# Dealing a tile's deep blocks over the whole batch, in a sparse graph attention on one core

## The chip, the core and the metric

The kernel runs on one core of a Trainium2 chip. The metric is the device time of one execution in microseconds; the median of three runs of the kernel before is 1906.26 us (1904.83 to 1914.43). TensorE (PE) does matrix products, VectorE (DVE) and ScalarE (ACT) elementwise work and reductions, GpSimd (POOL) issues indirect DMAs (gathers and scatters by a list of rows) and SyncE (SP) plain DMAs. Each engine runs its own list of instructions in the order in which the program emitted them and waits for the others by semaphores.

## What is computed

Attention over the edges of a graph, then the output projection, the residual and a layer norm, for 16 batches of 1024 nodes of 512 numbers, 8 heads of 64, all in fp32:

```python
q = (x @ Wq + bq).reshape(b, n, H, HD)
k = (x @ Wk + bk).reshape(b, n, H, HD)
v = (x @ Wv + bv).reshape(b, n, H, HD)
scores = einsum('bqhd,bkhd->bhqk', q, k) / sqrt(HD)
scores = scores + (1.0 - adj)[None, None] * -1e9
attn = softmax(scores, axis=-1)
out = einsum('bhqk,bkhd->bqhd', attn, v).reshape(b, n, d)
return layernorm(x + out @ Wo + bo)
```

`adj` (1024 x 1024, zeros and ones) is the same for all batches and very sparse: most nodes have a handful of edges, a few have dozens.

## The kernel before

**Tiles and blocks.** The nodes are sorted by their number of edges and cut into eight tiles of 128 queries, tile 7 having most edges. The kernel never makes the 1024 x 1024 scores. It works in *blocks* of 128 pairs of a query and a key. An *own* block i of tile t holds the i-th edge of each of its 128 queries; `OWN = (2, 1, 2, 3, 4, 5, 5, 7)` says how many each tile has. Edges beyond these are packed densely, 128 at a time, into *deep* blocks, `BLOCKS = (0, 0, 0, 0, 0, 0, 1, 5)`: tile 6 has one, tile 7 has five. Tiles 0 to 5 are called short here. Tile 1 (one key for each query) has no softmax to do and is handled apart; from the third batch on (`PAIRED_FROM = 2`) tile 0 is done once for two batches, in the odd one. So a batch has 34 blocks, or 32 in the even batches from 2 on, and the program has 530.

**What a block costs.** The list `blocks` fixes the order of all blocks, and one loop walks it, step n for block n, emitting for several blocks at once at different stages:

- `gather(n + 8)`: POOL gathers the K and V rows of the 128 keys (`kvg`, L1242, 128 x 1024); for a deep block also the 128 query rows (`qg`, L1196); at a tile's first block SP loads its query tile (`qt`).
- `products(n + 4)` (`qk`, L1263) and `scores(n + 4)` (`s`, L1267): VectorE multiplies Q and K and adds up by head.
- `exponentials(n + 3)` (`pv`, L1278): ScalarE.
- `weigh`: V times the exponentials, either on ScalarE as eight activations, one a head (L1291, at step n for block n + 2), or on VectorE as one operation (L1295, for block n + 1). `by_act(n)` decides. Own blocks after a tile's first always go to ScalarE; deep blocks go by turns (batch number plus i); a tile's first block goes by whether its place n in the list is even. The last 34 blocks go to VectorE where there is a choice.
- own blocks: `add_own(n)` (L1307), VectorE adds to the tile's running sum. Deep blocks: `add_up(n)`, two PE products with a matrix of zeros and ones (`sum`, L1316 and L1317) that send each edge to its query, accumulated in one pair of PSUM banks (a single buffer, `sum`) over the tile's deep blocks.
- `normalise(b, t)`, the closing of a tile: VectorE divides by the sum of exponentials (L1336, L1337), for tiles 6 and 7 after adding the `sum` buffer (L1328, L1329). Four PE transposes (`poT`, L1351), a copy by ScalarE (`oT`, L1355) and the output projection (`po`, L790) follow, then residual, layer norm and the store.

**The other work of the loop.** Meanwhile PE computes Q, K and V of the batches ahead, the *fronts*: transposes of x (`pxT`), products with Wq (`pq`), and K and V by a scheme with seven products in place of eight (`x`, `pp`, `z`, L947), whose results VectorE and ScalarE combine (L774 to L777 before the products, `e` L960, `w` L963, `g` L966, `kv` L970, L975, L979 and L826 after). K and V go to memory as rows, from which the gathers read; the Q rows likewise, into one of three buffers.

**What sets PE's share of a step.** Each step adds to a `credit`, and front or projection units are emitted while it lasts. `paced(share, n)` deals it over the steps of a batch in the ratio of `load_of(n)`, the planner's count of VectorE operations in the step: 2, plus 1 if the next block is weighed on VectorE, plus 1 for an own block that is not a tile's first, plus 1.3 at the step after a short tile closed or 3.0 after a deep one. An `add_up` takes `SUM` off the credit.

**The order before.** `blocks_of(b, t)` gives the order within a tile, and the list was simply tile after tile. For tile 6 that is 0 1 2 *5* 3 4, for tile 7 it is 0 1 *7* 2 *8* 3 *9* 4 *10* 5 *11* 6 (deep blocks slanted). So the five deep blocks of tile 7 all stood in the last 12 of a batch's 34 (or 32) blocks. A tile was closed at the step in which the next tile's block 0 came up. The one-key tile is turned at tile 7's own block 4, and its values are gathered at tile 7's block 0 (for the last batch both at tiles 2 and 3).

Of the kernel before, what the change touches and what calls it, by code (L numbers as in the profile page):

```python
# [26 lines left out]
OWN = (2, 1, 2, 3, 4, 5, 5, 7)  # L27
BLOCKS = (0, 0, 0, 0, 0, 0, 1, 5)
# [6 lines left out]
LONE, ONE_KEY, ONE_KEY_AT, ONE_KEY_LAST = 64, 1, (7, 4), (3, 0)  # L35
# [3 lines left out]
PAIRED_FROM, SPARED = 2, 56  # L39
# [138 lines left out]
def kernel(  # L178
# [37 lines left out]
    B, N, D = x.shape  # L216
    HD = D // HEADS
    NPAIR = D // P
    NT = N // P
# [34 lines left out]
    with ExitStack() as main:  # L254
# [82 lines left out]
        def merged(b):  # L337
            return b >= PAIRED_FROM and b % 2 == 1

        def tiles_of(b):  # L340
            return [t for t in range(NT) if t or b < PAIRED_FROM or merged(b)]
# [832 lines left out]
        def blocks_of(b, t):  # L1174

            own, deep = list(range(OWN[t])), list(range(OWN[t], OWN[t] + BLOCKS[t]))
            if b == 0 or not deep:
                return own + deep
            spread = max(1, len(own) // (len(deep) + 1))
            left = len(own) - spread * len(deep)  # L1180
            for j, i in enumerate(deep):
                own.insert(left + j * (spread + 1), i)
            return own

        blocks = [(b, t, i) for b in range(B) for t in tiles_of(b) if t != ONE_KEY for i in blocks_of(b, t)]
        start = [min(n for n, block in enumerate(blocks) if block[0] == b) for b in range(B)] + [len(blocks)]

        def load_more():
# [3 lines left out]
        def one_key_at(b):  # L1192
            return ONE_KEY_AT if b < B - 1 else ONE_KEY_LAST
# [71 lines left out]
        def scores(n):  # L1265
            S[n] = small.tile([P, HEADS], F32, tag="s", name=f"s_{n}", bufs=4)
            nc.vector.tensor_reduce(S[n], QK.pop(n).rearrange("p (h d) -> p h d", d=HD), axis=AX.X, op=OP.add)  # L1267
# [12 lines left out]
        def by_act(n):  # L1280
            b, t, i = blocks[n]
            if 0 < i < OWN[t]:
                return True
            turn_of = b + i if b and i else n
            return n < total - NBT and (turn_of % 2 == 0 or n < NBT // 2)
# [33 lines left out]
        def normalise(b, t):  # L1319
            pv = PV.pop((b, t))  # L1320
            o = work.tile([P, D], F32, tag="o", name=f"o_{b}_{t}", bufs=2)
            order_of = [u for u in tiles_of(b) if u != ONE_KEY]
            if t == order_of[0]:
                RDEN[b] = small.tile([P, NT - 1, HEADS], F32, tag="rden", name=f"rden_{b}", bufs=1)[:, 0:len(order_of), :]
            r = RDEN[b][:, order_of.index(t), :]
            if BLOCKS[t]:
                s = PSUM.pop((b, t))
                nc.vector.tensor_tensor(r, s[:, 1, HD2:HD2 + HEADS], pv[:, D:], op=OP.add)  # L1328
                nc.vector.tensor_tensor(  # L1329
                    o.rearrange("p (a d) -> p a d", a=2), s[:, :, 0:HD2], pv[:, 0:D].rearrange("p (a d) -> p a d", a=2),  # L1330
                    op=OP.add,
                )
                nc.vector.reciprocal(r, r)
                pv = o
            else:
                nc.vector.reciprocal(r, pv[:, D:])  # L1336
            nc.vector.tensor_tensor(  # L1337
                o.rearrange("p (h d) -> p h d", d=HD), pv[:, 0:D].rearrange("p (h d) -> p h d", d=HD),
                r[:, :, None].to_broadcast([P, HEADS, HD]), op=OP.mult,
            )  # L1340
            turn(b, t, o)
            if t == NT - 1:
                r = RDEN.pop(b)
                for k, op in enumerate((OP.min, OP.max)):
                    nc.vector.tensor_reduce(ends[:, k, b:b + 1], r, axis=AX.XY, op=op)

        def turn(b, t, o):
            def transpose():
                p = fill_psum(f"poT_{b}_{t}")
                for c in range(NPAIR):  # L1350
                    nc.tensor.transpose(p[:, ts(c, P)], o[:, ts(c, P)], ident)  # L1351

                def out():
                    OT[b, t] = work.tile([P, D], F32, tag="oT", name=f"oT_{b}_{t}", bufs=LAZY + 2)
                    nc.scalar.copy(OT[b, t], p)  # L1355
                    if number(b, t) in SPILL:
                        later(1, lambda: nc.sync.dma_start(spill[b * NT + t], OT.pop((b, t))))
                        spilled.append((b, t))
                    else:
                        later(1, lambda: done.append((b, t)))  # L1360

                later(1, out)

            later(1, lambda: urgent.append(transpose))
            if not fronts:
                coming.append((b, t))
# [67 lines left out]
        total = len(blocks)  # L1434
# [4 lines left out]
        def load_of(n):  # L1439

            b, t, i = blocks[n]
            had = 2.0 + (not by_act(min(n + 1, total - 1))) + (0 < i < OWN[t])
            if i == 0:
                had += 3.0 if BLOCKS[blocks[n - 1][1]] else 1.3
            return had

        def paced(share, n):
            if n >= total:
                return share
            b = blocks[n][0]  # L1450
            return share * load_of(n) * (start[b + 1] - start[b]) / sum(load_of(m) for m in range(start[b], start[b + 1]))
# [11 lines left out]
        with tc.manual_schedule():  # L1463
# [20 lines left out]
            n = -LEAD_IN  # L1484
            while n < total or plan or rest or urgent or done or finishing or spilled or lone_tiles or not guarded:
# [6 lines left out]
                elif n in start:  # L1492

                    b = start.index(n)
# [15 lines left out]
                    add_own(n)  # L1510
                if 0 <= n + 4 < total:
                    scores(n + 4)
                if 1 <= n <= total and (n == total or blocks[n][2] == 0):
                    normalise(*blocks[n - 1][:2])
                if 0 <= n < total and blocks[n][1:] == one_key_at(blocks[n][0]):
                    turn(blocks[n][0], ONE_KEY, V1.pop(blocks[n][0]))
                if 0 <= n < total and blocks[n] == (B - 1, *MORE_AT):
# [87 lines left out]
```

## Time and profile before

| | |
|---|---|
| median of three runs | 1906.26 us |
| the profiled execution | 1894.52 us, its span 1892.4 us |
| stretch from batch 1's closing to batch 14's | 394.9 to 1761.4 us |
| in it: PE, VectorE, ScalarE, POOL busy | 1338.6, 1272.7, 1196.4, 938.8 us |
| in it: DMA share | 0.88 |
| before and after that stretch | 394.9 us and 131.0 us |

All times that are read from the trace belong to the profiled execution, which is 0.6% shorter than the median. In its windows a line gives the stretch, its length, then for each engine the busy time and the count of instructions, the granted share of the TensorE clock, the busy share of the 16 DMA engines and what they moved. In lists of waits a line says which engine and instruction stood idle, what ended the idle time, and how much it was in all, how often, and the longest. The span's first part holds the setup, the ranking of the nodes and the packing of the edges; the middle stretch is the steady walk over thirteen batches; the last part has no fronts left.

### The profile page before, as it was taken

Reading aid. Unit: us, or ns where it says so; the run is one execution under the profiler, and the core shown is the slowest. Engines: PE = TensorE matmul, PEld = TensorE weight load, DVE = VectorE, ACT = ScalarE, POOL = GpSimd, SP = SyncE. Lnnn points to the kernel's source line nnn. Section 1 sums busy time; section 2 is a strip of 40 time slices with the busy share of each in tenths; the row PEclk is TensorE's granted clock in tenths of the full one; section 3 lists DMA queues with packets and bytes.
Section 4 is the critical chain, followed back from the end, with each engine's and each line's share of the span. In section 5 each row is a group of like instructions: output and inputs, shape, how many; then the busy total and the mean of one; then the engine's idle time right before and its main releaser. Section 6 shows DMA issues by size and latency. Waiting matters only on the chain. (4 is left out here: it accounts for less than half of the span.)

```text
span 1892.4 us, 25171 instructions
## 1 busy us (share of the span) xinstructions
PE 1816.5 (96%) x5149; PEld 876.6 (46%) x5149; DVE 1695.3 (90%) x3470; ACT 1557.4 (82%) x6128; POOL 1262.6 (67%) x1189
## 2 busy tenths in 40 slices
PE   7979999999999999999999999999999999999996
PEld 3434444444545454444444444444545444444442
DVE  6888879999998999899999989899999989997875
ACT  3627868988888988988898878988899989977885
POOL 1366765777676776767676766767676866656884
PEclk9989999999999999999999999999999999999998
DMA  7356786888989897989889897989889899989993
GB/s 279 115 167 215 226 290 229 309 298 291 322 266 319 303 333 256 345 290 310 299 284 329 279 324 261 334 303 309 286 302 352 297 332 319 329 282 319 340 332 137
DMA packets 188149, 544.63 MB, mean 288 GB/s; under 512 B 32602, under 2 KB 32622, under 8 KB 187986
## 3 DMA queue, kind: packets, MB, share of 16 engines
q0 software_dynamic: 116400, 382.82, 60.4%
q1 hardware_dynamic: 68510, 154.30, 21.7%
q10 hardware_dynamic: 3076, 5.82, 0.8%
q14 instruction: 120, 0.98, 0.2%
q8 instruction: 43, 0.70, 0.2%
HBM read 419.52 MB, written 144.34 MB: 298 GB/s over the span
## 5 line engine op out<-in xcount | busy, mean ns | idle before, releaser
L1291 ACT ACTIVATE pv<-kvg,pv 128x64 f32<-128x64 f32 x3544 | 893.4, 340 | 1.8 <-issue 1.8
L1242 POOL DMA_INDIRECT kvg<-kv_pair,place_row x462 | 522.6, 1131 | 258.6 <-issue 94.5
L790 PE MATMUL po<-wo,oT 128*128 128x512 f32 x816 | 379.2, 600 | 2.0 <-DVE vsum L854 1.2
L790 PE MATMUL pq<-wq,xT 128*128 128x512 f32 x792 | 369.4, 598 | 1.3 <-DVE s L1267 0.8
L1267 DVE TENSOR_REDUCE s<-qk 128x8 f32<-128x512 f32 x530 | 360.8, 681 | 7.2
L1263 DVE TENSOR_TENSOR qk<-qt,kvg 128x512 f32<-128x512 f32 x434 | 296.8, 684 | 13.2 <-DMA kvg<-kv_pair,place_row 13.1
L947 PE MATMUL x<-b,xT 128*128 128x512 f32 x504 | 239.0, 597 | 0.1
L947 PE MATMUL pp<-t,s 128*128 128x512 f32 x504 | 237.3, 593 | 1.5 <-DVE t L383 1.5
L1307 DVE TENSOR_TENSOR pv<-pv,pv 128x520 f32<-128x520 f32 x329 | 228.4, 694 | 8.2 <-ACT pv L1291 8.0
L790 PEld LDWEIGHTS po<-wo,oT 128*128 128x128 f32 x816 | 153.4, 192 | 171.7 <-issue 162.7
L790 PEld LDWEIGHTS pq<-wq,xT 128*128 128x128 f32 x792 | 149.0, 192 | 169.3 <-issue 157.7
L1001 POOL DMA_INDIRECT x<-in_x_dram,asked_row x120 | 129.6, 1080 | 103.5 <-PE pxT L748 35.4
L1278 ACT ACTIVATE pv<-s,absent 128x8 f32<-128x8 f32 x434 | 126.8, 293 | 55.1 <-DVE s L1267 36.6
L1125 POOL DMA_INDIRECT out_dram<-y,asked_row x129 | 145.1, 1125 | 35.9 <-issue 25.0
L800 ACT ACTIVATE sq_k<-kv 128x128 bf16<-128x128 f32 x512 | 150.8, 300 | 8.4 <-DVE kv L970 4.5
L947 PEld LDWEIGHTS x<-b,xT 128*128 128x128 f32 x504 | 95.3, 192 | 111.6 <-issue 105.2
L947 PEld LDWEIGHTS pp<-t,s 128*128 128x128 f32 x504 | 94.1, 190 | 111.3 <-issue 102.2
L947 PE MATMUL z<-b,s 128*128 128x512 f32 x252 | 121.4, 604 | 13.1 <-DVE kv L975 10.4
L1196 POOL DMA_INDIRECT qg<-q_rows,query_row x96 | 105.5, 1099 | 28.5 <-issue 25.3
L1029 POOL DMA_INDIRECT y<-in_x_dram,asked_row x93 | 105.0, 1129 | 26.1 <-issue 25.8
L947 PE MATMUL z<-t,s 128*128 128x512 f32 x252 | 118.6, 593 | 0.0
L947 PE MATMUL pp<-t,xT 128*128 128x512 f32 x252 | 118.5, 592 | 0.0
(276 smaller groups left out, 2750.2 us busy)
## 6 DMA issues: line engine op xcount, KB each, us to landing
kv_pair<-kv SPq DMA_DIRECT2D x98, 512.0 KB
q_rows<-q SPq DMA_DIRECT2D x106, 256.0 KB
qt<-q_rows SPq DMA_DIRECT2D x98, 256.0 KB
residual<-x SPq DMA_DIRECT2D x36, 256.0 KB
y<-residual SPq DMA_DIRECT2D x36, 256.0 KB
kv_rows<-kv SPq DMA_DIRECT2D x15, 512.0 KB
kvg<-kv_pair,place_row POOLq DMA_INDIRECT x462
kv_pair<-kv SPq DMA_DIRECT2D x28, 256.0 KB
```

Source lines behind the costliest of these rows:

```text
L790: nc.tensor.matmul(p, lhs(c), w[:, c, :], start=(c == 0), stop=(c == NPAIR - 1))
L800: nc.scalar.activation(sq, s[:, ts(h, P)], AF.Square, scale=scale, accum_out=sums[:, h:h + 1])
L947: nc.tensor.matmul(R[bank], l[:, ts(c, P)], right[:, c, :], start=(first and c == 0), stop=(c == 1), skip_group_check=True,)
L1001: nc.gpsimd.indirect_dma_start(out=y, out_offset=None, in_=x_rows, in_offset=bass.IndirectOffsetOnAxis(ap=asked_row[:, t:t + 1], axis=0), ...
L1125: nc.gpsimd.indirect_dma_start(out=out_rows[b, t], out_offset=bass.IndirectOffsetOnAxis(ap=rows, axis=0), in_=y, in_offset=None, element_o ...
L1196: nc.gpsimd.indirect_dma_start(out=q, out_offset=None, in_=q_rows[b % ROWS], in_offset=bass.IndirectOffsetOnAxis(ap=rows, axis=0))
L1242: nc.gpsimd.indirect_dma_start(out=KG[n], out_offset=None, in_=rows, in_offset=bass.IndirectOffsetOnAxis(ap=(place_row if b else key_row)[ ...
L1263: nc.vector.tensor_tensor(QK[n], q, KG[n][:, 0:D], op=OP.mult)
L1267: nc.vector.tensor_reduce(S[n], QK.pop(n).rearrange("p (h d) -> p h d", d=HD), axis=AX.X, op=OP.add)
L1278: nc.scalar.activation(PV[n][:, D:], S.pop(n), AF.Exp, bias=bias)
L1291: nc.scalar.activation(pv[:, ts(h, HD)], v[:, ds(D + h * HD, HD)], AF.Copy, scale=pv[:, D + h:D + h + 1])
L1307: nc.vector.tensor_tensor(PV[b, t], PV[b, t], pv, op=OP.add)
```

## The change

From batch 2 on the blocks of a batch are ordered by a new function. It lists the own blocks of the short tiles and then tile 7's seven own blocks (21, or 23 in odd batches), inserts tile 7's five deep blocks at equal distances into that list, and puts tile 6, in its old inner order, at the end. In an odd batch (tile.block, deep ones with a star):

```
before  0.0 0.1 2.0 2.1 3.0 3.1 3.2 4.0 4.1 4.2 4.3 5.0 5.1 5.2 5.3 5.4
        6.0 6.1 6.2 6.5* 6.3 6.4
        7.0 7.1 7.7* 7.2 7.8* 7.3 7.9* 7.4 7.10* 7.5 7.11* 7.6
after   0.0 0.1 2.0 7.7* 2.1 3.0 3.1 3.2 7.8* 4.0 4.1 4.2 4.3 7.9* 5.0 5.1 5.2 5.3 7.10* 5.4
        7.0 7.1 7.2 7.11* 7.3 7.4 7.5 7.6
        6.0 6.1 6.2 6.5* 6.3 6.4
```

Batches 0 and 1 keep their order. As a tile's block 0 no longer marks the closing of the tile before it, a table (`closes`) holds for each block whether it is a tile's last, and the closings, the planner's load and the check at a batch's last closing go by it.

```diff
-        blocks = [(b, t, i) for b in range(B) for t in tiles_of(b) if t != ONE_KEY for i in blocks_of(b, t)]
+        def batch_blocks(b):
+            tiles = [t for t in tiles_of(b) if t != ONE_KEY]
+            if b < PAIRED_FROM:
+                return [(b, t, i) for t in tiles for i in blocks_of(b, t)]
+            last = NT - 1
+            spread = [(b, t, i) for t in tiles if not BLOCKS[t] for i in range(OWN[t])]
+            spread += [(b, last, i) for i in range(OWN[last])]
+            n = len(spread)
+            for j in reversed(range(BLOCKS[last])):
+                spread.insert((j + 1) * n // (BLOCKS[last] + 1), (b, last, OWN[last] + j))
+            return spread + [(b, t, i) for t in tiles if BLOCKS[t] and t != last for i in blocks_of(b, t)]
+
+        blocks = [block for b in range(B) for block in batch_blocks(b)]
+        closing = {}
+        for n, (b, t, i) in enumerate(blocks):
+            closing[b, t] = n
+        closes = {n: tile_closed for tile_closed, n in closing.items()}
+        tiles_in_order = {b: [closes[n][1] for n in sorted(closes) if closes[n][0] == b] for b in range(B)}
...
-            order_of = [u for u in tiles_of(b) if u != ONE_KEY]
+            order_of = tiles_in_order[b]
...
-            if t == NT - 1:
+            if t == order_of[-1]:
...
-            if i == 0:
+            if n == 0 or n - 1 in closes:
                 had += 3.0 if BLOCKS[blocks[n - 1][1]] else 1.3
...
-                if 1 <= n <= total and (n == total or blocks[n][2] == 0):
-                    normalise(*blocks[n - 1][:2])
+                if n - 1 in closes:
+                    normalise(*closes[n - 1])
```

Nothing else is edited. What follows from the new numbering (which blocks a tile's first one by its even or odd place sends to ScalarE, which buffers a block takes) changes with it.

## The prediction

> **What bounds the kernel now.** I read four views in this order. First the page's busy shares.
>
> ```profile
> PE 1816.5 (96%) x5149; PEld 876.6 (46%) x5149; DVE 1695.3 (90%) x3470; ACT 1557.4 (82%) x6128; POOL 1262.6 (67%) x1189
> ```
>
> TensorE is busy nearly all the time, with VectorE and ScalarE close behind. A busy PE is not yet PE at its peak, so the second view counts work: the groups of PE in the stretch from batch 1's closing to batch 14's (394.9 to 1761.4 us). There stand 2684 records of fp32 products 512 wide; eight take 3.43 us where the chain of waits shows them back to back, so 0.429 us each, 1152 us. With 772 transposes at 0.109 (84 us), 156 pairs of `sum` products at 0.44 (69 us) and 19 us of small ones, PE needs 1324 us of 1366.5. Only 42 us can be won without touching PE's work.
>
> Third, the waits of PE in that stretch, the longest lines:
>
> ```profile
> PE z L947 <- DVE kv L975: 9.2, 4, 3.9
> PE poT L1351 <- DVE o L1337: 4.7, 3, 2.5
> PE pm L858 <- DVE vsum L854: 2.2, 2, 1.2
> PE pxT L748 <- DVE q L821: 1.6, 2, 0.8
> ```
>
> Columns: us in total, times, longest. Of 28 us shown, 23 end with VectorE; DMA ends none. Fourth, the table of windows, cut at the start of L1328, the first instruction of a deep tile's closing (two per batch): for batches 8 to 11 a line from tile 7's closing to tile 6's, then a line of tile 7's twelve blocks.
>
> ```profile
> core 0: us, PE busy (x) PEld busy (x) DVE busy (x) ACT busy (x) POOL busy (x), PEclk, DMA share, GB/s
> 1029.00:1099.10 70.10, 64.31 (x183) 30.10 (x182) 64.86 (x132) 60.51 (x241) 48.81 (x46) 1.00 0.83 278
> 1099.10:1134.90 35.80, 35.80 (x102) 18.35 (x101) 31.81 (x60) 28.01 (x116) 24.48 (x22) 0.95 0.95 334
> 1134.90:1204.50 69.60, 69.60 (x202) 33.10 (x201) 66.61 (x136) 63.65 (x261) 47.63 (x45) 1.00 0.85 287
> 1204.50:1240.20 35.70, 34.87 (x103) 17.73 (x102) 33.02 (x62) 33.49 (x141) 23.29 (x23) 1.00 0.93 335
> 1240.20:1304.40 64.20, 63.11 (x181) 29.79 (x180) 62.78 (x127) 56.41 (x221) 45.01 (x42) 1.00 0.87 295
> 1304.40:1341.00 36.60, 35.16 (x108) 18.29 (x107) 33.82 (x65) 32.92 (x138) 28.25 (x26) 1.00 0.95 334
> 1341.00:1411.70 70.70, 70.70 (x199) 33.21 (x198) 66.41 (x134) 61.98 (x243) 46.86 (x44) 1.00 0.82 283
> 1411.70:1445.50 33.80, 32.98 (x105) 17.48 (x104) 30.59 (x59) 33.16 (x147) 22.97 (x22) 1.00 0.98 353
> ```
>
> The reader is to see two regimes. Ahead of tile 6's closing VectorE is 93 to 98% busy and DMA at 0.82 to 0.87; in tile 7's blocks VectorE falls to 89 to 93% and DMA climbs to 0.93 to 0.98. PE's loss stands where the one turns into the other: of batch 8's 5.8 us without PE, 3.9 end just before tile 6 closes, and the clock row of 0.95 after it is another 1.8 us. The chain there runs through VectorE, waits, and only then gives PE its product:
>
> ```profile
> 1088.89 0.60 DVE s L1267
> 1089.49 2.82 issue
> 1092.37 0.44 DVE s L774
> ...
> 1097.19 0.61 DVE kv L975
> 1097.85 2.61 PE z L947 x4
> ```
>
> **What the Trainium skill says.** Perfetto Trace Analysis, "Optimization Strategy", says that where the most contended engine changes over a kernel, interleaving those regimes may improve it: that is this change's shape, and the windows show the two regimes. "Identifying the Most-Contended Engine" there says matmul busy time is no measure of the distance to peak; the trace agrees (windows of 70.70 us busy of 70.70 hold products that need a little less). TensorE: Matmul & The Clock Gate, "Architectural detail", says VectorE and ScalarE work strictly in order: `kv L975` above stands behind `s L774`, which starts 2.8 us late. The same page, "Why this matters for your kernels", warns of PE idle beyond about 3 us: the 3.9 us wait is followed by the 0.95 clock.
>
> **The change part by part**, from batch 2 on (14 of 16 batches).
>
> *Order.* Per batch 32 or 34 blocks, the same ones. Before: short tiles (14 or 16 blocks), tile 6 (6), tile 7 (12, its five deep blocks at every second place). After: short tiles and tile 7's seven own blocks with a deep block after every third or fourth, then tile 6. No instruction of PE, POOL or SP is added; PE's 42 us stay the ceiling.
>
> *PE.* The five pairs of `sum` products, 5 x 0.87 = 4.4 us, were inside 12 blocks and are spread over 26 or 28. Products of the next batches are dealt by VectorE load and each brings VectorE work after it; `sum` brings none. So the old tile 7 stretch had about 4.4 us less of such work, which is the slack in the windows. In numbers, for an odd batch of 34 blocks: PE needs 34 x 1324 / 428 = 105 us, dealt by load_of, whose values sum to 105.5. A unit of it is one VectorE operation of 0.61 us (their spacing on the chain), so the blocks take 64.4 us of VectorE, and the other 33.5 of its 97.9 (1272.7 / 13 batches) follow products: 0.336 us per us of PE that is not `sum` (99.7). Short tiles before: load 53.2, PE 52.9, VectorE 32.5 + 17.8 = 50.3, or 95% of PE's need; tile 6: 93%; tile 7: load 35, PE 34.8, VectorE 21.4 + 0.336 x 30.4 = 31.6, or 91%. After: the mixed part 63.2, PE 62.9, VectorE 38.6 + 20.0, 93%; the rest of tile 7 and tile 6 93% each. This estimate orders the regimes as the windows do; the swing of 4% goes.
>
> *Deep blocks' gathers.* Each has two on POOL: kvg 1.13 and qg 1.10 us. Ten within 12 blocks become ten within 26; the DMA share of 0.93 to 0.98 should go to about 0.88, the mean of the whole stretch. Gain: part of VectorE's 14.3 us on late kvg transfers, some 5 us of VectorE, nothing directly for PE. The first qg of a batch is now issued five blocks before the batch, and waits for that batch's q rows; these are written before the K and V rows for which the batch's first gather waits anyway, so it costs nothing. Should that cover fail, POOL's in-order queue (x, y, stores, powers) would stand behind it; I keep 5 us in the range for it. qt loads on SP keep their number; tile 6's moves twelve blocks later, tile 7's (and the one-key gather with it) two earlier, each still 8 blocks ahead of use: nothing.
>
> *Who weighs.* For first blocks of a tile the engine goes by the block's number, and numbers shift: in the seven even batches 2 to 14 one more block goes to ScalarE. VectorE loses 7 x 0.61 = 4.3 us, ScalarE gains 7 x 8 activations. The timeline shows eight in 1.91 to 2.02 us, so 13.6 us. ScalarE's idle in the stretch is 1366.5 - 1196.4 = 170 us, which hides it on average.
>
> *Closings.* Tile 7's comes six blocks before the batch's end and tile 6's at the end; the one-key tile's (at own block 4 of tile 7) four blocks earlier. The accumulator of `sum` has one buffer: tile 6's deep block now comes three blocks after tile 7's closing, some 9 us; the closing's two reads take under 1 us. The next batch's first deep block comes three after tile 6's closing. No wait added.
>
> *ScalarE's run.* This is the bad part. Own blocks after the first are always weighed by ScalarE, deep ones by turns. With deep blocks thinned and tiles 7 and 6 in a row, the longest run of blocks weighed by ScalarE alone grows from 14 to 18. Such a block needs 1.95 + 0.2 us, plus 0.97 of other ScalarE work (1196.4 us over 428 blocks is 2.80, less 0.85 x 2.15): 3.12 us beside PE's 1324 / 428 = 3.09. In the run ScalarE has no slack. Loss between 0 (PE has work queued) and 2 us in each of the 14 batches; I take 2 us in all.
>
> *Sum.* PE's waits on VectorE are 23 us, the lower clock after the long ones about 5 (three dips of 1.5 to 1.8). Of PE's gaps above 0.6 us in the timeline (26 us) some 19 stand near tile 6's end or in tile 7. I take half of those, 9.5, and half of the clock loss, 2.5, less 2 for ScalarE: 10 us. On the profiled execution, 1894.52 (span 1892.4 and 2 us around it), that is 1884.5; the median shown, 1906.26, lies 11.7 above it, so 1896.
>
> **Rivals.** *The gaps only move.* The blocks' own VectorE operations in a sliding stretch of 18 blocks are about as uneven after as before (own blocks and two heavy closings now crowd the batch's end), and PE is within 3% of its need. For it: PE at 70.70 of 70.70 us beside VectorE at 94%. Against it: the chance to smooth `sum` and gathers is real. Time 1906, plus or minus 6.
>
> *Slower: ScalarE's run binds.* Place: from tile 7's first own block to the next batch's first deep one. Price: 1.2 us more per batch than PE has queued, over 14 batches 17 us: 1923. It decides once other ScalarE work in the run exceeds 1.04 us a block, since 2.15 + 1.04 passes the 3.19 a block takes now (1366.5 / 428). For it: ScalarE already shows 33.16 of 33.80 us in batch 11's tile 7. Against it: runs of 14 exist now and PE shows no wait on ScalarE above 1.1 us.
>
> *More than half goes.* If level VectorE and DMA take nearly all of VectorE's part, 23 + 5 us go: 1878.
>
> **How the numbers follow.** The forecast has 0.45, gaps that move 0.21, ScalarE's run 0.26, the large gain 0.08. The forecast's own range is 1884 to 1903. 0.5% (9.5 us) is about what a measurement can tell from no change: some 0.12 of the forecast's chance falls within it, and 0.05 of the gaps that move ends on the slow side. Faster 0.41, same 0.28, slower 0.31. The range runs from the large gain to the slow rival, 1877 to 1924.
>
> **What would show it.** Right: PE's waits on `kv L975` and `o L1337` fall by half, VectorE's share differs less between stretches, DMA's row flattens, PE's count of work is unchanged. Wrong: ScalarE above 98% from tile 7's own blocks to the batch's end with PE waiting on e, kv or oT from ScalarE; or the same 42 us short of PE's need at other places.

## The result, and the profile after

The changed kernel takes 1888.84 us (median of six runs, 1884.68 to 1892.51), the kernel before beside it 1907.14 (six runs, 1904.83 to 1914.43): a ratio of 0.9896, interval 0.9868 to 0.9924, or some 20 us less. Run again later on another chip (`e9_changed_again` below) the ratio is 0.9932, interval 0.9907 to 0.9957, some 13 us. So the gain is about 0.7 to 1.0%, in the forecast's direction and larger than its 10 us; the time lies inside the range of 1884 to 1903 that the prediction gave.

The two profiled executions are not the middle of their kernels: that of the changed kernel took 1888.5 us (span 1886.7), that of the kernel before 1894.52, 12 us under its median; it is none of the six runs above. They differ by 6 us only, and the changed one lost 6 us before the steady stretch begins (400.8 us against 394.9), where the change touches nothing. What it does is read from the stretch between the closings of batch 1 and batch 14: 1355.0 us against 1366.5. What comes after is the same, 130.9 and 131.0 us.

The page's first part, busy time of each engine:

```profile
PE 1814.2 (96%) x5136; PEld 878.0 (47%) x5150; DVE 1687.8 (89%) x3462; ACT 1565.7 (83%) x6184; POOL 1264.1 (67%) x1189
```

ScalarE has 56 instructions more: seven weighings of eight activations, as counted. PE's work is the same: counted as in the prediction it needs 1326 us of the steady stretch, so the stretch is now 29 us longer than PE's need, where it was 42 us longer.

The waits of PE in that stretch of the changed kernel (us in total, times, longest), the five longest:

```profile
PE pm L858 <- DVE vsum L854: 3.3, 2, 1.9
PE z L947 <- DVE kv L975: 3.3, 1, 3.3
PE poT L1369 <- DVE o L1355: 3.0, 1, 3.0
PE sum L1334 <- DVE pv L1313: 1.7, 2, 1.4
PE poT L1369 <- issue: 1.2, 2, 0.7
```

The wait on `kv L975` went from 9.2 to 3.3 us, that on `o` (L1337, now L1355) from 4.7 to 3.0; all that end with VectorE from 23 to 13 us.

The windows of the changed kernel, cut at the closings of tile 7 and tile 6 in batches 8 to 11, columns as before. The long lines hold the mixed part of a batch, the short ones tile 6's blocks at its end; the first line is the whole steady stretch:

```profile
400.80:1755.80 1355.00, 1337.12 (x3826) 651.52 (x3833) 1266.68 (x2492) 1206.58 (x4882) 945.52 (x870) 1.00 0.90 309
1037.20:1119.00 81.80, 81.13 (x240) 40.01 (x240) 77.45 (x153) 74.57 (x300) 59.14 (x56) 1.00 0.92 315
1119.00:1139.00 20.00, 20.00 (x53) 9.34 (x52) 19.76 (x40) 17.17 (x72) 15.22 (x14) 1.00 0.90 313
1139.00:1222.90 83.90, 83.83 (x246) 41.26 (x246) 79.96 (x156) 75.69 (x313) 58.01 (x53) 1.00 0.89 311
1222.90:1240.00 17.10, 17.10 (x53) 8.52 (x52) 16.87 (x36) 17.10 (x69) 12.26 (x13) 1.00 0.87 289
1240.00:1320.50 80.50, 79.60 (x231) 38.91 (x230) 78.07 (x154) 74.84 (x305) 58.64 (x53) 1.00 0.90 313
1320.50:1339.60 19.10, 19.10 (x57) 9.49 (x56) 18.71 (x39) 17.77 (x73) 15.24 (x15) 1.00 0.90 310
1339.60:1428.90 89.30, 89.23 (x258) 43.58 (x258) 82.28 (x159) 78.06 (x323) 62.30 (x57) 1.00 0.89 311
1428.90:1446.40 17.50, 17.27 (x52) 8.52 (x51) 17.29 (x37) 17.50 (x73) 13.51 (x13) 1.00 0.94 343
```

DMA now lies between 0.89 and 0.92 in the long lines, where tile 7's stretch had 0.93 to 0.98: the gathers are spread. VectorE is not level: over these four batches it is busy 94.7% of the mixed part and 98.5% of tile 6's blocks. In the prediction's table the two regimes had 94.9 and 91.1%, so the difference is 3.8 points before and after. ScalarE fills tile 6's stretch of the odd batches to the last, 17.10 of 17.10 and 17.50 of 17.50 us, and PE lacks no more than 0.23 us there.

The gathers' lateness shows in the groups of VectorE. First the group of the kernel before, then the same group after (busy us, mean ns | idle us just before it, and what ended it):

```profile
L1263 DVE TENSOR_TENSOR qk<-qt,kvg 128x512 f32<-128x512 f32 x434 | 296.8, 684 | 13.2 <-DMA kvg<-kv_pair,place_row 13.1
```

```profile
L1281 DVE TENSOR_TENSOR qk<-qt,kvg 128x512 f32<-128x512 f32 x434 | 296.7, 684 | 0.0
```

VectorE's 13.1 us on late K and V rows are gone in this group. Whether this is what PE gained from is a question for the experiments.

Where PE's shortfall stands can be read by taking, for each step of batches 2 to 14, its length less PE's work in it. A step is cut here where VectorE starts `qk` for the block four ahead, and PE's work is counted with the prediction's times of one record, so these sums are estimates. Before, they come to 42 us: 18.1 in tile 6's steps, 12.0 in tile 7's, 12.1 in the short tiles'. After they are 30 us: 5.5, 12.7 and 11.4. In this pair of traces the gain stands in the steps of tile 6, which is dealt nothing and only moved to the end; tile 7's steps, wherever they now stand, lose as much as before. One line of windows of the kernel before shows it, from tile 5's closing to tile 6's in batch 8:

```profile
1074.60:1099.09 24.49, 19.47 (x55) 8.67 (x54) 21.33 (x44) 20.64 (x83) 19.41 (x20) 1.00 0.90 310
```

24.5 us for these blocks, 5.0 of them without PE; batch 8's tile 6 after the change has 20.00 us, with PE busy throughout.

### The profile page after: what moved, and what is told of

It is laid out like the page before. It is cut to its first block, busy times and chain, and to the rows that moved or that the text cites. A ratio compares the mean times of both kernels' runs of the same rounds, so it can differ in the third digit from the quotient of the medians.

```text
span 1886.7 us, 25241 instructions
## 1 busy us (share of the span) xinstructions
PE 1814.2 (96%) x5136; PEld 878.0 (47%) x5150; DVE 1687.8 (89%) x3462; ACT 1565.7 (83%) x6184; POOL 1264.1 (67%) x1189
## 4 chain that ended last, share of the span: by engine, by line
PE 64%; DVE 12%; ACT 9%; issue 5%; DMA 2%; POOL 2%; SPq 0%; another core or an unknown queue 0%; POOLq 0%; DVEq 0%; ACTq 0%
PE po L790 16%; PE pq L790 13%; PE pp L947 11%; PE x L947 8%; PE z L947 8%; ACT pv L1309 6%; PE poT L1369 2%; DVE qk L1281 2%; PE pxT L748 2%; DVE s L1285 2%; PE sum L1335 2%; PE sum L1334 2%; ACT sq_k L800 1%; DVE pv L1325 1%; POOL kvg L1260 1%
## 5 line engine op out<-in xcount | busy, mean ns | idle before, releaser
L1309 ACT ACTIVATE pv<-kvg,pv 128x64 f32<-128x64 f32 x3600 | 908.3, 342 | 0.9 <-issue 0.7
L790 PE MATMUL po<-wo,oT 128*128 128x512 f32 x816 | 374.4, 596 | 0.8 <-DVE g L966 0.3
L1214 POOL DMA_INDIRECT qg<-q_rows,query_row x96 | 109.9, 1145 | 27.9 <-issue 25.2
L1121 ACT ACTIVATE y<-y,stats 128x512 f32<-128x512 f32 (+1 forms) x129 | 103.8, 807 | 17.9 <-DVE stats L1116 14.4
```

The costliest lines, as they stand in the source:

```text
L790: nc.tensor.matmul(p, lhs(c), w[:, c, :], start=(c == 0), stop=(c == NPAIR - 1))
L1214: nc.gpsimd.indirect_dma_start(out=q, out_offset=None, in_=q_rows[b % ROWS], in_offset=bass.IndirectOffsetOnAxis(ap=rows, axis=0))
L1309: nc.scalar.activation(pv[:, ts(h, HD)], v[:, ds(D + h * HD, HD)], AF.Copy, scale=pv[:, D + h:D + h + 1])
```

## The experiments

Twelve kernels were timed, in three groups, each on a chip of its own. The kernel before took 1876.42, 1894.52 and 1896.76 us there, so only ratios to the kernel before on the same chip are compared; times that an expectation gives in microseconds stand beside the 1906 or 1907 us of the kernel before. Theories: the *levelling* of VectorE's need by dealing the deep blocks (the prediction's reason), *who weighs* (the blocks that change engine), and the *place of tile 6*. By the kernel's rule 19 blocks change engine. In the seven even batches 2 to 14 tile 4's first block goes to ScalarE; in the six odd ones 3 to 13 tile 5's first goes to ScalarE and tile 3's first to VectorE. The net is the seven weighings seen above.

**The change taken apart.** The first group splits it into its three parts: the dealing with the engines held as they were, the engines alone, and the order of tiles alone.

`e1_old_engines`, the changed kernel with each first block weighed where it was before:

```diff
+        old_blocks = [(b, t, i) for b in range(B) for t in tiles_of(b) if t != ONE_KEY for i in blocks_of(b, t)]
+        old_place = {block: n for n, block in enumerate(old_blocks)}
...
-            turn_of = b + i if b and i else n
+            turn_of = b + i if b and i else old_place[blocks[n]]
```

> The changed kernel, but every tile's first block is weighed on the engine that weighed it before (seven weighings go back from ScalarE to VectorE). If the gain comes from dealing the deep blocks (levelling), it stays near the changed kernel: 1888 to 1894, since 7 x 0.61 us of VectorE work is all that comes back. If the gain is that of the engines, it falls back to 1900 to 1907. If ScalarE's long run still costs something, it is faster than the changed kernel: 1880 to 1886.

Measured: 1866.84 us, ratio 0.9950 (0.9936 to 0.9963). Of 1907 us that would be 1898, between the expected ranges.

`e2_only_engines`, the kernel before with tile 4's first block of the seven even batches from 2 on given to ScalarE (the net seven; the changes of the odd batches are left out):

```diff
             turn_of = b + i if b and i else n
+            if b >= PAIRED_FROM and b % 2 == 0 and (t, i) == (4, 0):
+                turn_of = 0
```

> The kernel before with its order, but tile 4's first block of the seven even batches from 2 on weighed on ScalarE instead of VectorE. Levelling: at most the 4.3 us of VectorE work that goes, 1902 to 1907. Engines: most of the gain, 1889 to 1895.

Measured: 1873.86 us, ratio 0.9982 (0.9975 to 0.9989): 3.4 us, beside 4.3 us that VectorE was to lose. Together with `e1_old_engines` this makes 0.9950 x 0.9982 = 0.9932, which is what the changed kernel itself gave on the second chip.

`e3_tile6_last`, short tiles, then tile 7 in its old inner order, then tile 6, nothing dealt; the engines stay as before, since shifts by six and by twelve places keep even and odd:

```diff
-            spread = [(b, t, i) for t in tiles if not BLOCKS[t] for i in range(OWN[t])]
...
-            return spread + [(b, t, i) for t in tiles if BLOCKS[t] and t != last for i in blocks_of(b, t)]
+            order = [t for t in tiles if not BLOCKS[t]] + [last] + [t for t in tiles if BLOCKS[t] and t != last]
+            return [(b, t, i) for t in order for i in blocks_of(b, t)]
```

> The order short tiles, tile 7 in its old inner order (deep blocks at every second place), tile 6 last: only the tiles change places, nothing is dealt. Levelling: no gain, 1902 to 1910. If the place of tile 6 and of the two heavy closings is what helps: 1889 to 1896.

Measured: 1863.12 us, ratio 0.9925 (0.9911 to 0.9938). This is the run that decides. With nothing dealt and no engine changed it gains 0.75%. Its windows, in turn tile 7's twelve blocks, tile 6's, and the short tiles of the next batch:

```profile
1061.15:1093.80 32.65, 32.56 (x98) 16.87 (x97) 31.30 (x62) 28.00 (x113) 26.20 (x26) 1.00 0.95 338
1093.80:1113.70 19.90, 19.90 (x59) 9.84 (x58) 19.66 (x40) 17.07 (x73) 13.94 (x13) 1.00 0.96 345
1113.70:1165.62 51.92, 51.92 (x148) 24.36 (x147) 50.79 (x103) 47.51 (x189) 36.66 (x35) 1.00 0.87 296
1165.62:1198.44 32.82, 31.97 (x99) 16.59 (x98) 29.41 (x57) 30.60 (x135) 24.20 (x23) 1.00 0.95 328
1198.44:1216.17 17.73, 17.73 (x54) 8.90 (x53) 16.55 (x33) 17.04 (x73) 11.88 (x12) 1.00 0.86 286
1216.17:1262.97 46.80, 46.80 (x135) 22.45 (x134) 45.76 (x91) 42.35 (x166) 32.02 (x30) 1.00 0.89 305
```

The two regimes that the prediction saw are all there still: DMA at 0.95 in both of tile 7's stretches, VectorE at 90 and 96% in them and near 98% in the short tiles. Yet of these 201.82 us PE lacks 0.94, and its waits in the steady stretch are down to

```profile
PE poT L1365 <- DVE y L1099: 2.9, 2, 1.6
PE z L947 <- DVE kv L975: 2.7, 3, 1.3
PE poT L1365 <- DVE o L1351: 2.1, 1, 2.1
```

VectorE's waits on late `kvg` transfers are 1.0 us in this stretch, against 14.3 in the kernel before, so they nearly vanish without dealing too; `e1_old_engines`, with dealing, still has 4.9. That kernel, which has the dealing on top of the same last place of tile 6, is 0.25% slower. The intervals of the two ratios just touch, but both are taken against the same runs, and the five times of each (1865.86 to 1870.76 and 1862.37 to 1865.51) don't overlap: on this chip the dealing brought nothing and cost about 0.2%. Order and engines without dealing would be 0.9925 x 0.9982 = 0.9907, an estimate that was not run; it lies between the two measurements of the changed kernel.

On this chip the traces are less clear on where in the batch the gain stands than the first pair. PE's shortfall in `e2_only_engines`, which has the order of before, is 27.7 us, 7.4 of it in tile 6's steps; in `e3_tile6_last` it is 15.1, and 0.9. So about half of the 12.6 us between them stands in tile 6's steps, the rest in tile 7's (4.5) and the short tiles' (1.5).

`e4_bunched_early` has tile 6 last and tile 7's deep blocks close together near the batch's start:

```diff
-                spread.insert((j + 1) * n // (BLOCKS[last] + 1), (b, last, OWN[last] + j))
+                spread.insert(j + 2, (b, last, OWN[last] + j))
```

> The changed kernel's list, but tile 7's five deep blocks stand at places 2, 4, 6, 8 and 10 of the batch, among the short tiles, instead of at equal distances. Levelling: as uneven as before, only elsewhere, so little gain, 1900 to 1910. If it is enough that the deep blocks leave tile 7, wherever they go: 1886 to 1893.

Measured: 1872.66 us, ratio 0.9979 (0.9970 to 0.9988). It is inconclusive: the new numbering also sent a net 13 weighings from ScalarE to VectorE (its page has ACT x6024, the kernel before x6128), 13 x 0.61 = 7.9 us of VectorE, while seven moved the other way gave 3.4 us of time in `e2_only_engines`.

**Levelling without the order.** `e5_planner` is the kernel before, with 0.9 added to the planner's load of a deep block, so that more front work is dealt to tile 7's stretch, where VectorE had slack:

```diff
-            had = 2.0 + (not by_act(min(n + 1, total - 1))) + (0 < i < OWN[t])
+            had = 2.0 + (not by_act(min(n + 1, total - 1))) + (0 < i < OWN[t]) + 0.9 * (b >= PAIRED_FROM and i >= OWN[t])
```

> The kernel before with its order; only the planner's load of a deep block is 0.9 higher from batch 2 on, so that tile 7's stretch gets some 3 us more of the fronts' products and the other stretches less. Levelling of VectorE against PE (the prediction's estimate of 95, 93 and 91%): this alone levels it, ratio 0.990 to 0.995. If the swing of 4% did not matter: 0.998 to 1.002.

Measured: 1915.04 us, ratio 1.0104 (1.0076 to 1.0132). Slower than either expectation, and the slack is not taken up. Its windows for tile 7's blocks in batches 7 and 8:

```profile
1005.70:1044.30 38.60, 36.28 (x100) 18.63 (x101) 33.12 (x63) 30.73 (x128) 22.89 (x21) 0.91 0.89 313
1109.60:1149.40 39.80, 38.37 (x112) 19.47 (x111) 33.79 (x64) 28.77 (x119) 27.39 (x26) 1.00 0.95 339
```

VectorE stands at 86 and 85% there, less than before. PE's work in tile 7's steps, counted as above, rose from 466 to 482 us over the thirteen batches, less than half of the 3 us a batch that were meant. So this run shows that the planner's number is no remedy; it doesn't show what a full levelling would do. The timeline of PE at the first line's start (start, length, idle time before it and what ended it):

```profile
1000.13 1.88 PE L947 MATMUL pp<-t,xT 128*128 128x512 f32 x4
1008.02 3.78 PE L947 MATMUL z<-b,s 128*128 128x512 f32 x4 [6.02 <-DVE stats L1116]
```

PE waited 6 us for VectorE before it could go on with `z`. That more work dealt to a place makes PE's chain through VectorE and ScalarE denser there, and not shorter, is a reading of this line and not shown by a run of its own.

**The order varied.** `e7_tile6_first` puts tile 6 ahead of the short tiles and tile 7 last, `e8_tile7_first` puts tile 7 first and tile 6 last; nothing is dealt in either.

`e7_tile6_first`, as an edit of `e3_tile6_last`:

```diff
-            order = [t for t in tiles if not BLOCKS[t]] + [last] + [t for t in tiles if BLOCKS[t] and t != last]
+            short = [t for t in tiles if not BLOCKS[t]]
+            order = [6] + short + [7]
```

> Order tile 6, short tiles, tile 7 (old inner order), from batch 2 on. Read as a ring over the batches this is the same sequence as short, 7, 6; it only stands six blocks later against the batch's start, and so against the fronts, whose change from one batch to the next falls some 24 to 13 blocks before a batch's end. If the neighbourhood of the tiles is what helps (tile 7 straight after the short tiles, tile 6 straight after tile 7): ratio 0.991 to 0.994. If it is where the fronts' change of batch falls (before: on tile 6, whose blocks load ScalarE and VectorE most; with tile 6 last: on tile 7): here it falls on tiles 4 and 5, whose blocks are as heavy as tile 6's, so ratio 0.997 to 1.003.

Measured: 1896.71 us, ratio 1.0012 (0.9996 to 1.0028), in the range for the fronts' change of batch. Its profile says something else. The steady stretch is 1358.3 us, 8 less than in that of the kernel before and as short as the changed kernel's on the same chip (1359.5), but what follows it takes 139.4 us in place of 131.0. The gain of the steady stretch is given back at the end; why this order ends later was not followed up.

`e8_tile7_first`, as an edit of `e7_tile6_first`:

```diff
-            order = [6] + short + [7]
+            order = [7] + short + [6]
```

> Order tile 7 (old inner order), short tiles, tile 6: as a ring the same sequence as the kernel before (short, 6, 7), twelve blocks later against the batch's start. Neighbourhood: ratio 0.998 to 1.002. Fronts' change of batch: it now falls on tiles 2 to 4, which have light first blocks, so some gain, 0.993 to 0.998.

Measured: 1909.62 us, ratio 1.0087 (1.0057 to 1.0117); the steady stretch 1373.0 us, the end 144.8. Neither reading expected a loss. So it isn't enough that tile 6 stands last. A pattern fits the profiles at hand: where tiles 5 and 6, two runs of five own blocks, follow each other (before, and this one) the steady stretch is longer than where they don't. But the shortfall of `e8_tile7_first` stands in the steps of the short tiles (30 us) and of tile 7 (22) and not in tile 6's (7), so the pattern isn't shown to be the cause.

**What is late in tile 6.** The timeline of PE in the kernel before, at the 3.9 us stall of batch 8:

```profile
1090.39 1.88 PE L947 MATMUL z<-t,s 128*128 128x512 f32 x4
1092.10 1.88 PE L947 MATMUL pp<-t,xT 128*128 128x512 f32 x4
1097.85 2.61 PE L947 MATMUL z<-b,s 128*128 128x512 f32 x4 [3.86 <-DVE kv L975]
```

`z`, `pp` and `z` again stand with nothing between. This is the first pair of an even batch's fronts: tile 0 has its Q done with the odd batch, tile 1 needs none, so this pair alone has no Q products, and PE has only its chain of products, each waiting for what VectorE and ScalarE made of the one before. Of the steps of tile 6 that lose over 0.55 us in the trace of before, those in even batches, where the fronts have come to an even batch's first pair, lose 14 us together, those in odd ones 4.

VectorE was not only busy ahead of this stall; it stood idle itself:

```profile
1092.37 0.44 DVE L774 TENSOR_TENSOR s<-xT 128x256 f32<-128x256 f32 x1 [2.88 <-issue]
```

By the kernel's text `s L774` writes the next pair's first sum into a tile with one buffer, which this pair's first `z` reads, and that `z` ended at 1092.27. The profile names no releaser on this line. It does in the changed kernel, where the same wait came back once, in batch 3, ahead of the one wait on `kv` that is left. The fronts are at an odd batch's first pair there, which has Q products, but none between its two `z`:

```profile
566.34 0.42 DVE L774 TENSOR_TENSOR s<-xT 128x256 f32<-128x256 f32 x1 [3.87 <-PE z L947]
571.21 3.78 PE L947 MATMUL z<-b,s 128*128 128x512 f32 x4 [3.29 <-DVE kv L975]
```

So VectorE waited for PE to let go of `s` (named by the profile in the second place, inferred in the first), `kv L975` behind it in VectorE's list came later, and then PE waited for that. A second buffer for `s` was not tried.

`e10_filler` gives this pair four of tile 2's Q products between `z` and the product after it, and takes them from the next pair (the lines that give their rows the right number are left out here):

```diff
...
+            if b >= PAIRED_FROM and b % 2 == 0 and j == 0:
+                q1 = [
+                    (cost, fn, lambda: (b, 2) in XT)
+                    for cost, fn, _ in product(f"pq_{b}_2", lambda c: XT[b, 2][:, ts(c, P)], W["q"], lambda p: out_q(2, p))
+                ]
+            if b >= PAIRED_FROM and b % 2 == 0 and j == 1:
+                q0 = []
```

> The kernel before with its order; only in the fronts of even batches the four Q products of tile 2 are emitted one pair earlier, between the first z and p4 of pair 0 (tiles 0 and 1), which has no Q products of its own there. The waits of PE on kv L975 (9.2 us) stand in that pair, in the steps of tile 6. If the loss was this pair's chain x, e, w, g, z, kv, z running through VectorE and ScalarE while tile 6 loads them, with nothing for PE to do between: ratio 0.990 to 0.995, and the waits of z on kv L975 are gone. If tile 6's place acts in another way: 0.998 to 1.002.

Measured: 1893.06 us, ratio 0.9975 (0.9959 to 0.9991). Its waits of PE in the steady stretch, the longest two and that on `kv`:

```profile
PE pxT L748 <- DVE o L1345: 2.4, 1, 2.4
PE pxT L748 <- DVE q L822: 2.4, 2, 1.9
...
PE z L955 <- DVE kv L983: 0.9, 2, 0.5
```

The wait of `z` on `kv` fell from 9.2 us to 0.9, with the order as before. At the same place of batch 8 VectorE's `s L774` is again 2.88 us late, but the four Q products fill the time, and PE waits 0.45 us for `kv` in place of 3.86. The ratio lies between the two expected ranges: 0.25%, beside the changed kernel's 0.7 to 1.0%. So the pair without filler is a part of the cause, and only a part. Where the 0.25% stands can't be read from the profiles: the steady stretch takes 1365.6 us, about as in that of before, and other waits of PE have grown. The same edit on the changed kernel and on tile 6 last:

> The changed kernel with the same edit. If the new order already keeps that pair away from tile 6, the edit brings little: ratio to the kernel before 0.988 to 0.993, as the changed kernel alone. If dealing and filling add up: 0.985 or less.

> Tile 6 last, tile 7 in its old inner order, with the same edit. As tile 6 last alone gave 0.9925: 0.990 to 0.993 if the pair is already clear of tile 6, 0.987 or less if they add up. Beside the changed kernel with the edit it tells once more whether dealing the deep blocks is worth anything.

Measured: 1883.34 us, ratio 0.9927 (0.9905 to 0.9949), and 1883.97 us, ratio 0.9926 (0.9899 to 0.9954). Neither ratio differs clearly from that of the same order without the filler (0.9896 and 0.9932; 0.9925). That both orders had taken the filler's part already fits this, but isn't shown: in the first of the two PE has a new wait, four times behind the first `z` of an even batch, for the transposed x that the filler itself needs from ScalarE. It may hide a gain.

```profile
PE pq L790 <- ACT xT L752: 10.1, 4, 5.0
```

Dealt or not dealt, the two can't be told apart, though the first has the seven weighings on ScalarE too. Their edit is the one above; nothing else differs from the changed kernel and from `e3_tile6_last`.

`e13_early_19` lets the fronts run 19 steps ahead in place of 13 so that the pair meets earlier blocks than tile 6's:

```diff
-EARLY = 13
+EARLY = 19
```

> The kernel before with its order; the planner keeps the fronts six blocks further ahead (EARLY 19 instead of 13), so that the pair that starts a batch's fronts falls on tiles 3 to 5 instead of 5 to 7. If it is only the meeting with tile 6 that costs: ratio 0.990 to 0.996. If a heavy stretch of own blocks costs as much as tile 6 does: 0.998 to 1.003.

Measured: 1909.26 us, ratio 1.0058 (1.0035 to 1.0080), above both expected ranges. The loss stands ahead of the steady stretch, which begins at 409.6 us where that of `e10_filler`, on the same chip, begins at 397.0; the stretch itself takes 1368.7 us, about as long as in the profile of before. Its waits:

```profile
PE z L947 <- DVE kv L975: 7.9, 4, 4.1
PE pxT L748 <- DVE q L821: 4.9, 3, 2.5
PE pm L858 <- DVE vsum L854: 4.3, 3, 2.6
```

PE's wait on `kv` is about as long as before (7.9 us). Its two long ones, 2.6 and 4.1 us, stand in steps of tile 5 and of tile 6, so the pair was moved but not kept off tile 6 everywhere. The run shows no gain from the wider lead; it doesn't settle what meeting tile 6 costs.

**The changed kernel once more**, on the second chip, with no edit:

> The changed kernel, unaltered, so that it stands on one chip beside the next three. All theories: a ratio near 0.990 to the kernel before. If its ratio here is 0.993 or more, the place of tile 6 alone (0.9925 before) accounts for all of it; at 0.989 or less, dealing adds about 0.4% to it.

Measured: 1879.89 us, ratio 0.9932 (0.9907 to 0.9957). By its own mark, 0.993 or more, the place of tile 6 accounts for all of it. The interval lies on both sides of that mark, but doesn't reach down to 0.989, where dealing was to add something.

Not tried: tile 6 last with the seven weighings on ScalarE, by the estimate above some 0.991. No version that ran is shown to beat the changed kernel.

## Why the prediction was right in direction, and where its reason failed

- *What bounds the kernel.* Held. PE's work is unchanged, and what was won, 11.5 us of the steady stretch, came out of the 42 us that PE lacked; of the waits that were to fall by half, that on `kv` fell by two thirds and that on `o` by a third.
- *PE: "The swing of 4% goes".* This is the step that failed, as the reason of the gain. VectorE's share still differs by 3.8 points between the regimes, where 93% in both was forecast; tile 7's steps, where levelling was to act, lose as much as before (12.0 and 12.7 us); and `e3_tile6_last` deals nothing and has the gain. `e5_planner`, made to take up the slack by itself, costs 1%, though it moved less than half of the work it meant to. In the sum of this part VectorE's time is that of a mean batch (97.9 us) beside PE's of an odd one; for 34 blocks it is 101.1, which raises the three shares by about 3 points and leaves the swing. The Trainium skill (Perfetto Trace Analysis, "Optimization Strategy") says that interleaving may help where the most contended engine changes; in the prediction's windows PE stays at or near the top in both regimes (92 to 100% busy), and in these runs interleaving brought nothing beyond what the move of tile 6 gave. The prediction did list that move, under *Order*, and gave it no price of its own: that the direction came out right is owed to it, and in that to luck.
- *Deep blocks' gathers.* The DMA row flattened as said. VectorE's late `kvg` went entirely, 14.3 us for the 5 forecast, but it went nearly as far, to 1.0 us, where the gathers stayed bunched (`e3_tile6_last`), so it isn't shown to be the dealing's work.
- *Who weighs.* Held for the net of seven: 4.3 us of VectorE forecast, 3.4 us of time in `e2_only_engines`. The sum left it out as a term of its own; it is a sixth to a quarter of the gain. That in the odd batches two tiles' first blocks change places was not seen.
- *ScalarE's run*, both the 2 us taken and the slower rival at 1923: nothing of it showed. ScalarE is full in tile 6's stretch of the odd batches, as the rival had it, and PE lacks at most 0.23 us there; that the work queued for PE covers the run is the likely reason.
- *Closings.* Held: PE's `sum` products wait for `pv` (1.7 us, 1.3 before) and not for a closing's reads of their buffer.
- *Sum: 10 us.* The size came near in the two profiles, 11.5 us of the steady stretch, and was too small by the ratios, 13 to 20 us; but it didn't come by the terms of the sum. Half of the gaps near tile 6's end and in tile 7 was to go; in the estimate by steps tile 6's part fell from 18.1 to 5.5 us and tile 7's not at all. The clock's term was nearly right: before, three stretches of 3.4 us ran at half speed, a loss of 5.1 us; after, one of 6.8, a loss of 3.4, so 1.7 for the 2.5 taken. The 2 us for ScalarE did not show.

What stays open: why moving tile 6 between tile 7 and the next batch takes away about three times as much as the filler does, and why `e8_tile7_first` loses in the short tiles. That PE waits in the first pair because nothing fills its chain is shown (`e10_filler`). That tile 6's heavy run of own blocks is what makes the chain slow there is only argued, and VectorE's own wait for `s` is a rival that no run tests.

## What to carry to other kernels

Before explaining a change by an average that it evens out, ask whether a smaller change keeps the average uneven and has the same effect: here the order of two tiles alone gave a gain of 0.75%, and the dealing on top of it none. When an engine is 3% short of its need, look for the few steps in which a chain of dependent products has no independent work between its links; here filling such a place (0.25%) or taking work off VectorE (0.18%) was worth more than levelling VectorE over a batch. And look whether the helper that is late was itself waiting for a buffer. Choices that go by a block's number move with every reorder, so hold them fixed in an experiment, or the experiment measures them too.

## What was not expected of the hardware

The kernel before took 1876.42, 1894.52, 1896.76 and 1907.14 us (medians) on the occasions it was timed, a spread of 1.6% that is larger than the effect studied, where its runs on one occasion lie within 0.5 to 1.1% of each other; times from different occasions say nothing of kernels. The Trainium skill (TensorE: Matmul & The Clock Gate, "Why this matters for your kernels") says to avoid gaps of PE beyond about 3 us, since they lower the clock. In the steady stretch of the two profiles the waits beyond that came with half speed (3.86 us before, 3.29 after; windows there read a granted clock of 0.50), but so did two shorter ones before, of 2.67 and 2.46 us, while one of 2.99 us after did not: here 3 us is no safe limit. `e5_planner` shows the price on one line: after the wait of 6.02 us four records of products took 3.78 us, where the four ahead of it took 1.88, and the clock of the stretch reads 0.91.
